# A two-layer relational graph network: memsets of 200 and 100 floats behind the gathers, one tile of 64 fetched row by row from SyncE, and another order of layer 1's last steps

## The chip, the cores and the metric

The kernel runs on one core of one Trainium2 chip. The metric is the device time of one execution, in microseconds (us), as the median over several runs. The engines of the core are PE (TensorE, matrix products), ACT (ScalarE), DVE (VectorE), POOL (GpSimd) and SP (SyncE, which here only issues DMAs). Each engine takes its instructions in program order and waits on semaphores for the others.

## What is computed

There are 12500 nodes with 128 features each and 200000 edges, sorted by destination; each edge has a source, a destination and one of 8 relation types. Two layers of a relational graph convolution are followed by a residual addition and a layer norm:

```python
def _rgcn_conv(x, src, dst, et, basis, comp, root, bias):
    W = jnp.einsum('rb,bio->rio', comp, basis)
    xw = jnp.einsum('ni,rio->nro', x, W)
    msgs = xw[src, et]
    seg = dst * N_REL + et
    summed = jax.ops.segment_sum(msgs, seg, num_segments=N_NODES * N_REL)
    cnt = jax.ops.segment_sum(jnp.ones((msgs.shape[0],), x.dtype), seg, num_segments=N_NODES * N_REL)
    mean = summed / jnp.maximum(cnt, 1.0)[:, None]
    agg = mean.reshape(N_NODES, N_REL, HIDDEN).sum(axis=1)
    return agg + x @ root + bias
...
h = x
for l in range(N_LAYERS):
    h = jax.nn.relu(_rgcn_conv(h, src, dst, et, basis[l], comp[l], root[l], bias[l])) + h
return _layernorm(x + h, axis=-1)
```

## The kernel before

The edges are cut into T = 1563 tiles of 128 edges, the tiles into NQ = 391 quads of four, and two quads make a group of eight tiles (NG = 196 groups). The 98 blocks of 128 nodes are the other measure of progress: about four quads feed one block.

**Layer 1** gathers, for each edge, its source's row of x (512 bytes). One indirect DMA on POOL brings the 128 rows of a tile (L583 in the function `gather`). PE multiplies each gathered tile with a one-hot matrix that DVE has written (`onehot`, L873; it holds the edges' weights too), which gives per-destination means transposed (`means`, L914); ACT copies them out. Per group PE applies the eight relation weights (`product`, L938) and places the result at its nodes (`place`, L961). When a block has all its edges, `close_block` adds the bias, takes the relu and the residual (L974 and after) and puts three steps on the list `todo`: a transposition, stored as hT_d, and two `half` steps that multiply the block with four of layer 2's relation weights each (L986). The products are stored as y_d, one row for each node and relation; both halves of a block are stored in one DMA. All these stores and loads are issued by SP (L565).

**Layer 2** gathers, for each edge, one row of y_d, by the index idy = source * 8 + type. PE multiplies the gathered tile with a one-hot matrix of 256 columns and accumulates straight into the block's sum (`add_rows`, L1028), to which it adds the root term. `finish` takes bias, relu and residual, `norm` transposes the block back and normalises it (L1062 to L1069), and SP stores the output. The gathers of layer 2 wait for all stores of y_d (L595).

**The memset.** Behind each gather POOL clears a part of a scratch tile `pace` (L589): 256 floats for each partition in layer 1, 200 in layer 2. Nothing reads it. Before that it waits for its own memset of eight gathers earlier.

**Order of the work.** The program is a list that is written out by hand: `Plan.add` takes each operation with the cells that it reads and writes, and derives the semaphore waits. Each engine executes its share of the list in that order, so an instruction that waits holds up everything behind it on its engine. The order comes from the loops over q at L1117 (layer 1) and L1166 (layer 2): in step q the gather of quad q + 12 is put on the list first (AHEAD = 12), into a ring of 14 quads, then DVE's one-hot of quad q + 2, then PE's work for quad q. The gathers use three lanes of semaphores in turn, the DMAs of SP eight. In the first part of layer 1 there is other work beside: DVE counts the edges per destination and type (`counts`, in pieces spread over the first steps) and computes the weights of layer 2.

After the loop of layer 1 stand its last steps (L1148 to L1158): place and close the last group but one, the product of the last group, the remaining `todo`, place and close the last block, its `todo`. The PSUM bank `pt` serves the transpositions and both halves of all blocks.

At the end SP waits for all DMAs, the engines meet (L1185, with a drain of each engine), each loads a flag `bad` (L1212), and a branch leads to another path for other inputs (L1213), which isn't taken here.

Of the kernel before, what the change touches and what calls it, by code (L numbers as in the profile page):

```python
# [8 lines left out]
F32 = mybir.dt.float32  # L9
# [3 lines left out]
ALU = mybir.AluOpType  # L13
# [402 lines left out]
def ordered_path(  # L416
# [21 lines left out]

    nc = tc.nc
    P = 128
    N, D = x.shape
# [16 lines left out]
    C = P + 2 * HALO  # L460
    S4 = 4
    AHEAD = 12
    H = R // 2
    assert D == P and R * K == P and B == BF + 1 and 1 < TL and LAST < P and BF % 4 == 0
    main = slice(HALO, HALO + P)

    const = ctx.enter_context(tc.tile_pool(name="const", bufs=1))
# [3 lines left out]
    def keep(shape, dtype, name):  # L471
        return const.tile(shape, dtype, name=name)
# [31 lines left out]
    sel = keep([P, G, K], F32, "sel")  # L504
    spread = keep([P, B, GB], F32, "spread")

    PACE, PACED = 8, (2 * P, 200)
    pace = keep([P, PACE, 2 * P], F32, "pace")
    paced = tc.alloc_semaphore("s_paced")
    key = keep([P, 4, C], F16, "key")  # L510
    low = keep([P, 4, C], I32, "low")
    eqs = Ring(const, 2, [P, S4, 4, C], F16, "eq")
    turns = Ring(const, 3, [P, 4, P], F32, "tu")
    rows_r = Ring(const, AHEAD + 2, [P, Q, D], F32, "rows")
    dm_r = Ring(const, 4, [P, Q, 2 * P], F32, "dm")
    sT_r = Ring(const, 3, [P, R, G, K], F32, "sT")
    pl_r = Ring(const, 3, [P, 2 * P], F32, "pl")
# [27 lines left out]
    o2 = keep([P, B], F32, "o2")  # L545
    nb_f = keep([1, 1], F32, "nb_f")

    plan = Plan(tc, {"hw": 8, "aq": 4, "gq": 3})
    plan.seen, plan.last = {}, {}

    def vec(emit, reads=(), writes=()):
# [5 lines left out]
    def pe(emit, reads=(), writes=()):  # L557
        plan.add("PE", emit, reads, writes)
# [8 lines left out]
    def copy(out_t, in_t, reads, writes):  # L567
        act(lambda: nc.scalar.activation(out_t, in_t, AF.Copy), reads, writes)  # L568

    rows_g = {}  # L570

    def gather(l, q):
        if q >= NQ:
            return
        t, cell = rows_r.take()
        rows_g[l, q] = (t, cell)
        ids = idx if l == 0 else idy

        def emit():
            ins = []  # L580
            for i in range(q * Q, min((q + 1) * Q, T)):
                m = LAST if i == T - 1 else P
                ins.append(nc.gpsimd.indirect_dma_start(  # L583
                    out=t[:m, i - q * Q, :], out_offset=None, in_=x if l == 0 else y_d,
                    in_offset=bass.IndirectOffsetOnAxis(ap=ids[:m, i:i + 1], axis=0)))
                k = l * T + i
                if k >= PACE:
                    nc.gpsimd.wait_ge(paced, k - PACE + 1)
                nc.gpsimd.memset(pace[:, k % PACE, :PACED[l]], 0).then_inc(paced, 1)  # L589
            return ins  # L590

        b = q * Q // P
        reads = ["idx0" if l == 0 and q == 0 else ("idx", b)] if l == 0 else [("idy", b)]
        if l == 1 and q == 0:
            reads += [("y_d", j) for j in range(NT)]  # L595
        plan.add("POOL", emit, reads, [cell], lane="gq", n=min(Q, T - q * Q))

    def weight(l, r):
        c0 = (l * R + r) * NB
# [280 lines left out]
    def load_block(j):  # L880
        if j >= NT:
            return
        n = rows_of(j)
        t, c = h_in[j] = hin_r.take()
        load(t[:n], x[j * P:j * P + n, :], [], [c])
# [20 lines left out]
    def means(q):  # L906
        t, c = rows_g.pop((0, q))
        d, dc = dms.pop((0, q))
        s, sc = s_b[q % 2]

        def emit():
            for i in range(in_quad(q)):
                m = LAST if q * Q + i == T - 1 else P
                last = nc.tensor.matmul(s[:, i, :], t[:m, i, :], d[:m, i, :P], start=True, stop=True)  # L914
            return last

        pe(emit, [c, dc], [sc])
        g = q * Q // G
        if g not in sT:
            sT[g] = sT_r.take()  # L920
        o, oc = sT[g]
        k0 = q * Q - g * G
        n = in_quad(q)
        copy(o[:, :, k0:k0 + n, :].rearrange("p r t k -> p t r k"),
             s[:, :n, :].rearrange("p t (r k) -> p t r k", k=K), [sc], [oc + (q % 2,)])
# [43 lines left out]
    def close_block(j):  # L969
        n = rows_of(j)  # L970
        p, pc = po[j]
        t, c = h_in.pop(j)
        h, hc = h_r.take()
        vec(lambda: nc.vector.tensor_add(h[:n], p[:n], bias_sb[:n]), [pc, "bias"], [hc])  # L974
        vec(lambda: nc.vector.scalar_tensor_tensor(h[:n], h[:n], 0.0, t[:n], op0=ALU.max, op1=ALU.add), [c], [hc])
        pt, pc2 = pt_b
        yc, ycc = yc_r.take()
        yr, yrc = yr_r.take()

        def turn():  # L980
            pe(lambda: nc.tensor.transpose(pt[:, 0, :n], h[:n, :], ident[:n, :n]), [hc, "ident"], [pc2])
            copy(yc[:, :n], pt[:, 0, :n], [pc2], [ycc])
            load(hT_d[j * P:(j + 1) * P, :n], yc[:, :n], [ycc], [("hT_d", j)])

        def half(k):
            pe(lambda: nc.tensor.matmul(pt[:n].rearrange("p r d -> p (r d)"), yc[:, :n],  # L986
                                        w_sb[:, 1, k * H:(k + 1) * H, :].rearrange("p r d -> p (r d)"),
                                        start=True, stop=True),
               [ycc] + [("w", 1, r) for r in range(k * H, (k + 1) * H)], [pc2])
            copy(yr[:n, k * H:(k + 1) * H, :], pt[:n], [pc2], [yrc + (k,)])  # L990
            if k == 1:
                load(y_d[j * P * R:(j * P + n) * R, :].rearrange("(p r) d -> p (r d)", r=R),
                     yr[:n].rearrange("p r d -> p (r d)"), [yrc + (0,), yrc + (1,)], [("y_d", j)])

        todo.extend([turn, lambda: half(0), lambda: half(1)])
# [7 lines left out]
             (ct_b[0].rearrange("p t d -> p (t d)")[:, :2 * P], ct_b[1])]  # L1003

    def load2(k):
        if not 0 <= k < NT:
            return
        n = rows_of(k)
        t, c = hTs[k] = hin_r.take()
        load(t[:, :n], hT_d[k * P:(k + 1) * P, :n], [("hT_d", k)], [c])  # L1010
        t, c = xs[k] = xs_r.take()
        load(t[:n], x[k * P:k * P + n, :], [], [c])

    def add_rows(q, k, opens, last):
        t, c = rows_g.pop((1, q))
        d, dc = dms.pop((1, q))
        a, ac = acc[k]
        n = in_quad(q)
        root_in = opens and k >= 0
        reads = [c, dc]  # L1020
        if root_in:
            ht, hc = hTs[k]
            reads += [hc, ("w", 1, R)]

        def emit():
            for i in range(n):
                m = LAST if q * Q + i == T - 1 else P
                ins = nc.tensor.matmul(a, t[:m, i, :], d[:m, i, :], start=(opens and i == 0),  # L1028
                                       stop=(last and i == n - 1))
                if i == 0 and root_in:  # L1030
                    nc.tensor.matmul(a[:, :rows_of(k)], w_sb[:, 1, R, :], ht[:, :rows_of(k)], start=False, stop=False)
            return ins

        pe(emit, reads, [ac])
# [60 lines left out]
        gather(0, q)  # L1095
    load_block(0)
    load_block(1)
    run(counts(0), 99)
    sources(*groups[1])
    turn_block(0)  # L1100
# [13 lines left out]
    later = [lambda b=b: check_edges(b) for b in range(B)]  # L1114
    later += [check_span, check_place, check_all]
    later.reverse()
    for q in range(NQ):  # L1117
        g = q * Q // G
        gather(0, q + AHEAD)
        onehot(0, q + 2)  # L1120
        if q == 1:
            where()
        if q % 2 == 0 and g > 0:
            place_in(g - 1)
        means(q)
        if q % 2 == 0:
            if g > 0:
                for j in fresh(g - 1):
                    open_block(j)
                product(g - 1)  # L1130
        else:
            if g > 0:
                for j in place(g - 1):
                    close_block(j)
            for j in fresh(g):
                if j not in hT:
                    turn_block(j)
                load_block(j + 1)
        if q % 4 != 3 and todo:
            todo.pop(0)()  # L1140
        if q < R:
            weight(1, q)
        if parts is not None:
            if run(parts, 2):
                parts = None
        elif later:
            later.pop()()
    g = NG - 1  # L1148
    for j in place(g - 1):
        close_block(j)  # L1150
    product(g)
    place_in(g)
    while todo:
        todo.pop(0)()
    for j in place(g):
        close_block(j)
    while todo:
# [2 lines left out]
    for q in range(AHEAD):  # L1160
        gather(1, q)
    load2(0)
    for q in range(2):
        onehot(1, q)
    due = []
    for q in range(NQ):  # L1166
        k = sup(q)
        gather(1, q + AHEAD)
        onehot(1, q + 2)
        opens = q == 0 or sup(q - 1) != k  # L1170
        last = q == NQ - 1 or sup(q + 1) != k
        if opens:
            acc[k] = acc_b[k % 3]
            load2(k + 1)
        add_rows(q, k, opens, last)
        for d in due:
            norm(d)
        due = []
        if last:
            finish(k)  # L1180
            due.append(k)
# [60 lines left out]
```

## Time and profile before

| | |
|---|---|
| median of 10 runs | 4499.05 us (4497.73 to 4502.11) |
| profiled execution | 4500.36 us; span of its instructions 4498.5 us |
| busy: POOL | 3929.1 us (87%) |
| busy: PE, its weight loads | 2758.6 us (61%), 2135.6 us (47%) |
| busy: DVE, ACT | 1711.0 us (38%), 518.7 us (12%) |
| DMA traffic | 295.88 MB, 66 GB/s |
| layer 1's gathers | first issued at 3.6 us, last at 2265.9 us |
| layer 2's gathers | first issued at 2289.8 us, last at 4470.2 us |

The profile is of one execution. In a group of instructions a row gives line, engine, operation, tiles written and read, shape, the count, then the busy time, the mean duration in ns, and the idle time of the engine just before them with what ended it ("issue" means that the engine waited for nothing that the profile shows). In order of time a row gives the start in us, the duration, the engine and, in brackets, the idle time ahead. "SPq" is SP's issuing of a DMA, not the transfer. In the list of waits the numbers are total us, times, and the longest. A row of one line's instructions gives shortest, median and longest duration in ns.

### The profile page before, as it was taken

What the parts mean: (1) busy time and instruction counts of PE and PEld (TensorE: products, weight loads), DVE (VectorE), ACT (ScalarE), POOL (GpSimd) and SP (SyncE); (2) the same over time, 40 slices, a digit from 0 to 9 for tenths busy, and PEclk for the clock granted to TensorE, in tenths of its full rate; (3) what the DMA queues carried; (4) which work ended last, traced back from release to release, by engine and by line L of the source; (5) the groups of instructions that cost most, each with busy time, mean ns of one, the idle gap of its engine ahead of it and who ended that gap; (6) DMA issues with size and microseconds to landing.
All of it is one profiled execution on the core that took longest, in us unless ns stands there. A gap on an engine that the chain in (4) does not pass through costs nothing.

```text
span 4498.5 us, 38109 instructions
## 1 busy us (share of the span) xinstructions
PE 2758.6 (61%) x11691; PEld 2135.6 (47%) x11691; DVE 1711.0 (38%) x4724; ACT 518.7 (12%) x1190; POOL 3929.1 (87%) x6260
## 2 busy tenths in 40 slices
PE   4786666666666666666665565565655556555554
PEld 3565555555555555555544344444444444444443
DVE  8772222222222222222234444444444444444343
ACT  0231211122111111121110000000000000000000
POOL 8888888888888888888878888888888888888886
PEclk7998888878888878888867766666667666666676
DMA  3222222222222222222222222222222222222221
GB/s 90 68 87 75 76 75 75 75 75 74 71 75 75 75 75 75 75 74 72 75 64 56 56 56 56 56 56 56 56 56 56 56 56 56 56 56 56 56 57 43
DMA packets 193416, 295.88 MB, mean 66 GB/s; under 512 B 60725, under 2 KB 130687, under 8 KB 193203
## 3 DMA queue, kind: packets, MB, share of 16 engines
q0 software_dynamic: 100032, 205.00, 17.5%
q1 hardware_dynamic: 90650, 86.62, 5.9%
q8 instruction: 96, 1.57, 0.2%
q10 hardware_dynamic: 2521, 1.73, 0.1%
q14 instruction: 117, 0.96, 0.1%
HBM read 229.11 MB, written 64.00 MB: 65 GB/s over the span
## 4 chain that ended last, share of the span: by engine, by line
POOL 72%; issue 10%; PE 9%; DVE 4%; DMA 4%; ACT 0%; POOLq 0%; ACTq 0%; DVEq 0%; SPq 0%
POOL rows L583 55%; POOL pace L589 17%; PE y L938 3%; DMA rows<-in_x_dram,idx 2%; PE s L914 2%; PE s L1028 2%; DMA rows<-y_d,idy 1%; DVE w_sb L607 1%; DVE dm L873 1%; PE ct L1028 1%; DVE eq L709 1%; PE ct L715 1%; PE ct L716 1%; PE pt L986 0%; DVE tu L732 0%
## 5 line engine op out<-in xcount | busy, mean ns | idle before, releaser
L583 POOL DMA_INDIRECT rows<-y_d,idy x1563 | 1486.9, 951 | 280.5 <-issue 254.8
L583 POOL DMA_INDIRECT rows<-in_x_dram,idx x1563 | 1495.4, 957 | 259.0 <-issue 250.3
L1028 PE MATMUL s<-dm,rows 128*128 128x256 f32 x2086 | 838.2, 565 | 595.7 <-DMA rows<-y_d,idy 444.7
L914 PE MATMUL s<-dm,rows 128*128 128x128 f32 x3126 | 539.5, 326 | 712.6 <-DMA rows<-in_x_dram,idx 712.1
L1028 PEld LDWEIGHTS s<-dm,rows 128*128 128x128 f32 x2086 | 558.3, 284 | 840.5 <-issue 459.5
L589 POOL MEMSET pace<- 128x256 f32 (+1 forms) x3126 | 953.0, 305 | 2.0
L914 PEld LDWEIGHTS s<-dm,rows 128*128 128x128 f32 x3126 | 466.9, 227 | 893.7 <-DMA rows<-in_x_dram,idx 760.9
L873 DVE TENSOR_SCALAR dm<-cols,near,w 128x256 f32<-128x256 f32 x1563 | 725.8, 533 | 56.7 <-PE ct L1028 28.8
L873 DVE TENSOR_SCALAR dm<-cols,kr,w 128x128 f32<-128x128 f32 x1563 | 531.3, 401 | 467.4 <-PE s L914 467.4
L1028 PE MATMUL ct<-dm,rows 128*128 128x256 f32 x1040 | 417.9, 565 | 307.5 <-DMA rows<-y_d,idy 231.5
L938 PE MATMUL y<-w_sb,sT 128*128 128x128 f32 x3136 | 566.6, 358 | 0.0
L938 PEld LDWEIGHTS y<-w_sb,sT 128*128 128x128 f32 x3136 | 557.8, 275 | 0.3 <-issue 0.2
L1028 PEld LDWEIGHTS ct<-dm,rows 128*128 128x128 f32 x1040 | 279.3, 285 | 429.9 <-issue 223.2
L974 DVE TENSOR_TENSOR h<-po,bias_sb 128x128 f32<-128x128 f32 x98 | 28.5, 290 | 947.3 <-PE po L961 947.3
L568 ACT ACTIVATE sT<-s 128x512 f32<-128x512 f32 x391 | 233.3, 597 | 1187.8 <-PE s L914 1187.8
L1047 DVE TENSOR_TENSOR y_col<-s,hT 128x128 f32<-128x128 f32 x66 | 19.2, 290 | 601.8 <-ACT hT L1040 601.8
L986 PE MATMUL pt<-w_sb,y_col 128*128 128x512 f32 x392 | 210.7, 620 | 2.1 <-ACT y_row L568 1.4
L1063 DVE TENSOR_TENSOR h<-po,xs 128x128 f32<-128x128 f32 x98 | 28.5, 291 | 308.3 <-PE po L1062 308.3
L1040 ACT ACTIVATE hT<-s,bias_t 128x128 f32<-128x128 f32 x65 | 23.9, 367 | 994.4 <-PE s L1028 994.4
L568 ACT ACTIVATE y_row<-pt 128x512 f32<-128x512 f32 x196 | 117.0, 597 | 140.9 <-PE pt L986 140.9
L961 PE MATMUL po<-ys,pl 128*128 128x128 f32 x780 | 119.7, 276 | 5.0 <-DVE pl L949 2.9
L1047 DVE TENSOR_TENSOR y_col<-ct,hT 128x128 f32<-128x128 f32 x32 | 9.3, 291 | 291.9 <-ACT hT L1040 291.9
(121 smaller groups left out, 1300.0 us busy)
## 6 DMA issues: line engine op xcount, KB each, us to landing
y_d<-y_row SPq DMA_DIRECT2D x97, 512.0 KB
rows<-in_x_dram,idx POOLq DMA_INDIRECT x1563
rows<-y_d,idy POOLq DMA_INDIRECT x1563
h_in<-in_x_dram SPq DMA_DIRECT2D x98, 64.0 KB
h_in<-hT_d SPq DMA_DIRECT2D x98, 64.0 KB
xs<-in_x_dram SPq DMA_DIRECT2D x98, 64.0 KB
hT_d<-y_col SPq DMA_DIRECT2D x97, 64.0 KB
out_dram<-ys SPq DMA_DIRECT2D x97, 64.0 KB
```

The source lines that it names most:

```text
L568: act(lambda: nc.scalar.activation(out_t, in_t, AF.Copy), reads, writes)
L583: ins.append(nc.gpsimd.indirect_dma_start(out=t[:m, i - q * Q, :], out_offset=None, in_=x if l == 0 else y_d, in_offset=bass.IndirectOffse ...
L589: nc.gpsimd.memset(pace[:, k % PACE, :PACED[l]], 0).then_inc(paced, 1)
L607: vec(lambda b=b: nc.vector.scalar_tensor_tensor(w_sb[:, l, r, :], b_sb[:, l, b, :], comp_sb[:, c0 + b:c0 + b + 1], w_sb[:, l, r, :], op0= ...
L709: vec(lambda s=s, eq=eq, s0=s0: nc.vector.tensor_tensor(eq[:, s - s0, :nb, HALO - s:HALO + P], key[:, :nb, HALO - s:HALO + P], key[:, :nb, ...
L715: nc.tensor.matmul(ct[:, :nb, :], id_h, eq[:, s - s0, :nb, main], start=(s == 1), stop=False)
L873: last = nc.vector.tensor_scalar(t[:, i - q * Q, :wide], cols[:, :wide], ids[:, i:i + 1], w[:, i:i + 1], op0=ALU.is_equal, op1=ALU.mult)
L914: last = nc.tensor.matmul(s[:, i, :], t[:m, i, :], d[:m, i, :P], start=True, stop=True)
L938: last = nc.tensor.matmul(y[:m], t[:, r, :nt, :].rearrange("p t k -> p (t k)"), w_sb[:, 0, r, :], start=(r == 0), stop=(r == R - 1))
L961: last = nc.tensor.matmul(po[j][0][:n], t[:m, k * P:k * P + n], o[:m], start=False, stop=(j in closed))
L986: pe(lambda: nc.tensor.matmul(pt[:n].rearrange("p r d -> p (r d)"), yc[:, :n], w_sb[:, 1, k * H:(k + 1) * H, :].rearrange("p r d -> p (r d)"),
L1028: ins = nc.tensor.matmul(a, t[:m, i, :], d[:m, i, :], start=(opens and i == 0), stop=(last and i == n - 1))
```

## The change

The memsets shrink from 256 to 200 floats in layer 1 and from 200 to 100 in layer 2.

One tile in 64 (tiles 63, 127, ..., 1535; 24 a layer) is no longer gathered by POOL. SP fetches its 128 rows, one DMA for each row: in each step q, `fetch` loads eight source numbers from `src_i` into eight registers of SP and issues eight DMAs of one row each ("a bite"); sixteen bites make a tile. The bite of step q belongs to the quad eight steps later (LEAD), the first eight bites of each layer stand ahead of its loop, and each waits for the bite four before it on its lane. The tile lies in a ring of two. PE's matmul of that tile reads this ring instead of `rows`. After the loop of layer 1 one DVE operation turns `src_i` into source * 8 + type for 1536 tiles; layer 2's bites load these numbers.

In the last steps of layer 1, the product, placing and closing of the last group but one, and the `todo` steps except one, now come before the means of the last quad (which the loop leaves out). For the last block only, the second half is multiplied into the bank `ct` instead of `pt` and copied by DVE instead of ACT, and each half is stored by its own DMA.

In layer 2 the loads of block 1 are put ahead of the loop, a drain of POOL is put behind the last gather, and in the last step the normalisation of the last block but one comes before the last quad's matmuls.

```diff
     AHEAD = 12
+    FAR, LEAD = 16, 8
+    BITE = P // FAR
     H = R // 2
-    assert D == P and R * K == P and B == BF + 1 and 1 < TL and LAST < P and BF % 4 == 0
+    assert D == P and R * K == P and B == BF + 1 and 1 < TL and LAST < P and BF % 4 == 0 and NQ % 2 == 1
     main = slice(HALO, HALO + P)
...
-    PACE, PACED = 8, (2 * P, 200)
+    PACE, PACED = 8, (200, 100)
     pace = keep([P, PACE, 2 * P], F32, "pace")
     paced = tc.alloc_semaphore("s_paced")
+    n_paced = [0]
     key = keep([P, 4, C], F16, "key")
...
     rows_r = Ring(const, AHEAD + 2, [P, Q, D], F32, "rows")
+    far_r = {e: Ring(const, 2, [P, D], F32, f"far{e}") for e in ("SP", "ACT")}
     dm_r = Ring(const, 4, [P, Q, 2 * P], F32, "dm")
...
-    plan = Plan(tc, {"hw": 8, "aq": 4, "gq": 3})
+    plan = Plan(tc, {"hw": 8, "aq": 4, "gq": 3, "rSP": 4, "rACT": 4})
+    far_at = {"SP": FAR - 1}
+    row_regs = {e: [plan.engines[e].alloc_register(f"row{k}") for k in range(BITE)] for e in far_at}
     plan.seen, plan.last = {}, {}
...
-    rows_g = {}
+    rows_g, far_g = {}, {}
+
+    def far(i):
+        for e, at in far_at.items():
+            if i % (FAR * Q) == at * Q + Q - 1 and i < BF * P and (at == FAR - 1 or i >= FAR * Q):
+                return e
+        return None
+
+    def fetch(e, l, q, part=0, parts=1):
+
+
+        s = q + LEAD + FAR - 1 - far_at[e]
+        i, c = (s // FAR * FAR + far_at[e]) * Q + Q - 1, s % FAR
+        if far(i) != e:
+            return
+        if c == 0 and part == 0:
+            far_g[l, i] = far_r[e].take()
+        t, cell = far_g[l, i]
+        n = BITE // parts
+        eng = plan.engines[e]
+        regs = row_regs[e]
+
+        def emit():
+            if part == 0:
+                eng.load(regs, src_i[i % P:i % P + 1, i // P, c * BITE:(c + 1) * BITE])
+            ins = []
+            for k in range(part * n, part * n + n):
+                at = eng.snap(regs[k], min_val=0, max_val=(N if l == 0 else N * R) - 1)
+                p = c * BITE + k
+                ins.append(eng.dma_start(t[p:p + 1, :], (x if l == 0 else y_d)[bass.ds(at, 1), :]))
+            return ins
+
+        reads = [("src", i // P)]
+        if l == 1 and i < 2 * FAR * Q:
+            reads += [("y_d", j) for j in range(NT)] + [("y_d", NT - 1, 1)]
+        plan.add(e, emit, reads, [cell + (c, part)], lane="r" + e, n=n)
+
+    def bits(l, i):
+        return [far_g[l, i][1] + (c, part) for c in range(FAR) for part in range(2)] if far(i) else []
...
+        tiles = [i for i in range(q * Q, min((q + 1) * Q, T)) if not far(i)]
+
...
             ins = []
-            for i in range(q * Q, min((q + 1) * Q, T)):
+            for i in tiles:
                 m = LAST if i == T - 1 else P
...
                     in_offset=bass.IndirectOffsetOnAxis(ap=ids[:m, i:i + 1], axis=0)))
-                k = l * T + i
+                k = n_paced[0]
+                n_paced[0] += 1
                 if k >= PACE:
...
         if l == 1 and q == 0:
-            reads += [("y_d", j) for j in range(NT)]
-        plan.add("POOL", emit, reads, [cell], lane="gq", n=min(Q, T - q * Q))
+            reads += [("y_d", j) for j in range(NT)] + [("y_d", NT - 1, 1)]
+        plan.add("POOL", emit, reads, [cell], lane="gq", n=len(tiles))
...
                 m = LAST if q * Q + i == T - 1 else P
-                last = nc.tensor.matmul(s[:, i, :], t[:m, i, :], d[:m, i, :P], start=True, stop=True)
+                rows = far_g[0, q * Q + i][0] if far(q * Q + i) else t[:, i, :]
+                last = nc.tensor.matmul(s[:, i, :], rows[:m], d[:m, i, :P], start=True, stop=True)
             return last
-        pe(emit, [c, dc], [sc])
+        pe(emit, [c, dc] + bits(0, q * Q + Q - 1), [sc])
         g = q * Q // G
...
         def half(k):
-            pe(lambda: nc.tensor.matmul(pt[:n].rearrange("p r d -> p (r d)"), yc[:, :n],
+            hb, hc2 = ct_b if j == NT - 1 and k == 1 else pt_b
+            pe(lambda: nc.tensor.matmul(hb[:n].rearrange("p r d -> p (r d)"), yc[:, :n],
                                         w_sb[:, 1, k * H:(k + 1) * H, :].rearrange("p r d -> p (r d)"),
                                         start=True, stop=True),
-               [ycc] + [("w", 1, r) for r in range(k * H, (k + 1) * H)], [pc2])
-            copy(yr[:n, k * H:(k + 1) * H, :], pt[:n], [pc2], [yrc + (k,)])
+               [ycc] + [("w", 1, r) for r in range(k * H, (k + 1) * H)], [hc2])
+            if j == NT - 1:
+                if k == 0:
+                    copy(yr[:n, :H, :], hb[:n], [hc2], [yrc + (k,)])
+                else:
+                    vec(lambda: nc.vector.tensor_copy(yr[:n, H:, :], hb[:n]), [hc2], [yrc + (k,)])
+                load(y_d[j * P * R:(j * P + n) * R, :].rearrange("(p r) d -> p r d", r=R)[:, k * H:(k + 1) * H, :],
+                     yr[:n, k * H:(k + 1) * H, :], [yrc + (k,)], [("y_d", j) if k == 0 else ("y_d", j, 1)])
+                return
+            copy(yr[:n, k * H:(k + 1) * H, :], hb[:n], [hc2], [yrc + (k,)])
             if k == 1:
...
     def load2(k):
-        if not 0 <= k < NT:
+        if not 0 <= k < NT or k in hTs:
             return
...
         root_in = opens and k >= 0
-        reads = [c, dc]
+        reads = [c, dc] + bits(1, q * Q + Q - 1)
         if root_in:
...
                 m = LAST if q * Q + i == T - 1 else P
-                ins = nc.tensor.matmul(a, t[:m, i, :], d[:m, i, :], start=(opens and i == 0),
+                rows = far_g[1, q * Q + i][0] if far(q * Q + i) else t[:, i, :]
+                ins = nc.tensor.matmul(a, rows[:m], d[:m, i, :], start=(opens and i == 0),
                                        stop=(last and i == n - 1))
...
     load_block(1)
+    for s in range(LEAD):
+        fetch("SP", 0, s - LEAD)
     run(counts(0), 99)
...
     later.reverse()
-    for q in range(NQ):
+    for q in range(NQ - 1):
         g = q * Q // G
         gather(0, q + AHEAD)
+        fetch("SP", 0, q)
         onehot(0, q + 2)
...
             later.pop()()
+    srcs = [("src", b) for b in range(BF)]
+    vec(lambda: nc.vector.scalar_tensor_tensor(src_i[:, :BF], src_i[:, :BF], float(R), ex[:, :BF, main], op0=ALU.mult,
+                                               op1=ALU.add),
+        ends("ex", 0, BF) + [("ex", 0, n) for n in (1, 2, 3)] + srcs, srcs)
     g = NG - 1
+    while todo:
+        todo.pop(0)()
+    place_in(g - 1)
+    for j in fresh(g - 1):
+        open_block(j)
+    product(g - 1)
     for j in place(g - 1):
         close_block(j)
+    place_in(g)
+    while len(todo) > 1:
+        todo.pop(0)()
+    means(NQ - 1)
+    todo.pop(0)()
     product(g)
-    place_in(g)
-    while todo:
-        todo.pop(0)()
     for j in place(g):
...
     load2(0)
+    load2(1)
+    for s in range(LEAD):
+        fetch("SP", 1, s - LEAD)
     for q in range(2):
...
         gather(1, q + AHEAD)
+        if q + AHEAD == NQ - 1:
+            pool(lambda: nc.gpsimd.drain())
+        fetch("SP", 1, q)
         onehot(1, q + 2)
...
             load2(k + 1)
-        add_rows(q, k, opens, last)
+        if q < NQ - 1:
+            add_rows(q, k, opens, last)
         for d in due:
...
         due = []
+        if q == NQ - 1:
+            add_rows(q, k, opens, last)
         if last:
...
             due.append(k)
```

## The prediction

> **What bounds the kernel now.** I read the page first (busy time, then the chain that ended last), then the groups of instructions with their shapes kept apart, then POOL in order of time.
>
> ```profile
> span 4498.5 us, 38109 instructions
> POOL 72%; issue 10%; PE 9%; DVE 4%; DMA 4%; ACT 0%; POOLq 0%; ACTq 0%; DVEq 0%; SPq 0%
> L583 POOL DMA_INDIRECT rows<-in_x_dram,idx x1563 | 1495.4, 957 | 259.0 <-issue 250.3 <-PE y L938 6.1 <-DMA idx<-in_src_dram 1.6
> L583 POOL DMA_INDIRECT rows<-y_d,idy x1563 | 1486.9, 951 | 280.5 <-issue 254.8 <-DMA y_d<-y_row 22.6 <-PE po L1062 3.1
> L589 POOL MEMSET pace<- 128x256 f32 x1563 | 513.5, 329 | 1.0
> L589 POOL MEMSET pace<- 128x200 f32 x1563 | 439.5, 281 | 1.0
> PE s L914 <- DMA rows<-in_x_dram,idx: 712.1, 290, 4.4
> PE s L1028 <- DMA rows<-y_d,idy: 444.7, 194, 3.8
> ```
>
> The chain is POOL for 72%, with most of the 10% "issue" between POOL's instructions. PE waits for gathered rows in both layers (712 and 445 us), so it follows the gathers. POOL's work is one strict alternation; in order of time, a piece of layer 1 and a piece of layer 2:
>
> ```profile
> 1000.18 0.95 POOL L583 DMA_INDIRECT rows<-in_x_dram,idx  x1 [0.17 <-issue]
> 1001.13 0.33 POOL L589 MEMSET pace<- 128x256 f32 x1
> ...
> 3000.19 0.95 POOL L583 DMA_INDIRECT rows<-y_d,idy  x1 [0.17 <-issue]
> 3001.14 0.28 POOL L589 MEMSET pace<- 128x200 f32 x1
> 3001.59 0.95 POOL L583 DMA_INDIRECT rows<-y_d,idy  x1 [0.17 <-issue]
> ```
>
> The gather takes 0.95 us and the idle time ahead of it 0.17 us, whether 256 or 200 floats are cleared between. The memset is therefore paid in full: a tile costs 957 + 329 + 166 (259.0 / 1563) = 1452 ns in layer 1, and 951 + 281 + 165 ((280.5 - 22.6) / 1563) = 1397 ns in layer 2.
>
> **The change, part by part.** All sums are against the profiled execution (4500.36 us; its span is 4498.5); the median of the ten runs, 4499.05, lies 1.3 us lower, which is taken off at the end. A difference of 0.2% (9 us) is about the least that a measurement of this kernel tells from none.
>
> *Memsets.* From 256 to 200 floats the duration falls by 48 ns; from the rows' busy times, (513.5 - 439.5) / 1563 = 47.3 ns for 56 floats, 0.845 ns a float. At 200 in layer 1 the row is there: 281 ns. At 100 no row exists; the nearest below is a memset of one float:
>
> ```profile
> 0.24 0.10 POOL L1228 MEMSET const-float32-0.0<- 128x1 f32 x1 [0.24 <-issue]
> ```
>
> So the bounds are 100 and 281 ns; the line through 256 and 200 gives 281 - 84.5 = 197 ns, and ends at 113 ns for one float, near the 100 measured, so I take 197. Layer 1 saves 1539 x 47.3 ns = 73 us, layer 2 1539 x 84.5 ns = 130 us (1539 gathers a layer remain). If nothing is given back elsewhere these lie on the chain.
>
> *One tile of 64 off POOL.* Tiles 63, 127, ..., 1535 are 24 in each layer. POOL loses 24 x 1.452 = 35 us and 24 x 1.397 = 34 us. SP gains, for each quad of tiles, one register load and eight DMAs of one row. The rows of SP that come nearest:
>
> ```profile
> 0.96 0.45 SPq L565 DMA_DIRECT2D idx<-in_src_dram  x1
> 1.46 0.40 SPq L565 DMA_DIRECT2D ex<-in_edge_type_dram  x1
> 4.27 0.26 SPq L565 DMA_DIRECT2D src_i<-in_src_dram  x1
> L1212 SPq TENSOR_LOAD <-bad x1: 462/462/462, 4491.7 to 4491.7; - x1
> L1212 SPq FUSED_REGOPS  x1: 191/191/191, 4496.3 to 4496.3; - x1
> L1212 SPq SEQ_ASSERT  x1: 32/32/32, 4496.5 to 4496.5; - x1
> ```
>
> The second and third are DMAs of one row each (704 and 256 bytes): 0.26 to 0.40 us, with about 0.05 us to the next (0.96 + 0.45 to 1.46). No row shows a DMA whose address sits in a register. From below its addition is nothing, from above a register operation and an assertion each time, 0.22 us. The load of eight registers lies between one load of one register, 0.46 us, and eight of them, 3.7 us. A "bite" of eight rows thus costs between 8 x 0.31 + 0.46 = 2.9 us and 8 x (0.45 + 0.05 + 0.22) + 3.7 = 9.5 us. I take 4.2: eight times (0.33 + 0.05 + 0.05) plus 0.8, because the row's offset is one scaling of a register and the eight numbers lie side by side. What else SP does for a block of 128 nodes:
>
> ```profile
> 1008.36 0.32 SPq L565 DMA_DIRECT2D y_d<-y_row  x1
> 1008.73 0.43 SPq L565 DMA_DIRECT2D h_in<-in_x_dram  x1
> ...
> 2335.13 0.34 SPq L565 DMA_DIRECT2D out_dram<-ys  x1
> 2335.51 0.43 SPq L565 DMA_DIRECT2D h_in<-hT_d  x1
> 2335.99 0.43 SPq L565 DMA_DIRECT2D xs<-in_x_dram  x1
> ```
>
> About 1.3 us a block, 130 us a layer. With 384 bites of 4.2 us a layer is 1613 + 130 = 1743 us of SP, against some 2020 us of gathers in the new layer 2 (1539 x 1.313). SP is then 86% full, and a bite is issued eight quads (over 40 us) ahead of its use, so it stays hidden. Queued behind a bite on SP are the stores of y_d, hT_d and the outputs and the loads of h_in and xs; each comes up to 4 us later. At the start of layer 2 eight bites stand together (34 us): loads for the third block come late there and PE may fall behind by some 10 to 20 us, but POOL fills its ring of 14 quads meanwhile (72 us of gathers), and PE's waits leave room to catch up. PE's extra wait for the bites comes once in 16 quads. Cover gone, this is the first rival.
>
> *The start of layer 1.* There POOL is not alone on the path. The windows of the gathered rows' tile, first 240 us:
>
> ```profile
> core 0: us, PE busy (x) PEld busy (x) POOL busy (x), PEclk, DMA share, GB/s
> 0.00:240.00 240.00, 30.14 (x208) 29.29 (x208) 158.07 (x159) 0.86 0.28 77
> ```
>
> 159 gathers are out and PE has used 104 tiles (two matmuls each): a lead of 55 in a ring that holds 56. A faster POOL meets the end of the ring, and what it gained by then, 159 x 47 ns + 2 tiles x 1.45 us = 10 us, is lost. I charge 10 us.
>
> *Layer 1's last steps.* POOL in order of time, and pieces of the chain of waits between:
>
> ```profile
> 2266.84 0.33 POOL L589 MEMSET pace<- 128x256 f32 x1
> 2289.77 0.96 POOL L583 DMA_INDIRECT rows<-y_d,idy  x1 [22.60 <-DMA y_d<-y_row]
> ...
> 2265.92 2.39 DMA rows<-in_x_dram,idx
> 2269.48 3.42 PE y L938 x16
> 2283.38 2.02 PE pt L986 x2
> 2286.04 2.98 DMA y_d<-y_row
> ```
>
> POOL idles 22.6 us. The product of 3.4 us, with the placing and closing behind it, waits behind the last quad's matmuls on PE; after the change it goes ahead of them, into time in which PE waited for the rows. The very last block's second half goes to another PSUM bank and to DVE, so one ACT copy (0.6 us) leaves the chain. PE's work stays and is now the chain, so I take 3.3 us, between 0 and 6. New there is one DVE operation on 1536 columns:
>
> ```profile
> L736 DVE SCALAR_TENSOR_TENSOR tu<-src_i,ex 128x512 f32<-128x512 int32 x3 | 2.0, 662 | 0.0
> ```
>
> Three times 0.66 us is 2 us, while DVE waits for PE; it costs nothing unless a last gather is held up for as long.
>
> *The end.* The drain of POOL, and who waits for it:
>
> ```profile
> 4471.15 0.28 POOL L589 MEMSET pace<- 128x200 f32 x1
> L1185 POOLq DRAIN  x1: 8477/8477/8477, 4483.1 to 4483.1; - x1
> SPq L1185 <- POOLq L1185: 8.3, 1, 8.3
> ```
>
> POOL is idle from 4471.4 to 4483.1 and then drains for 8.5 us with everything waiting. The change drains behind the last gather; 4471.4 + 8.5 = 4479.9 is before 4483.1, so 8.3 us go, if the second drain finds nothing left (0 to 8.3). Moving the last block but one's normalisation ahead of the last matmuls is worth 1 us at most; I take 1.
>
> **Sum.** Layer 1: 73 + 35 - 10 = 98. Between layers 3. Layer 2: 130 + 34 = 164. End 9. Together 274 us: 4500.4 - 274 = 4226, less 1.3 for the median: 4225 us.
>
> **Rivals.**
>
> *SP becomes the bound (slower).* In-order SP sets the pace once 384 bites and 130 us exceed layer 2's 2020 us: from 4.9 us a bite. At 5.0 the layer takes 2050 us, the kernel some 4255. At 6.0 both layers take 384 x 6.0 + 130 = 2434 us, with 40 us of ends 4910 us. It equals the kernel before at about 5.5. For it: the bounds (2.9 to 9.5) straddle the point, and nothing shows the register-addressed form. Against: the short one-row DMAs, and that most of a bite is plain issue. A little over the line (4.9 to 5.4 us): 0.06; beyond: 0.11. [...] No run here shows a load of several registers.
>
> *The memset hides work of POOL.* If something behind the gather takes as long as the 446 ns (281 + 165) that now follow it in layer 2, a shorter memset only lengthens the idle time or the gather. Then layer 2 gives back 130 us (4355 us), and if the same holds at 256, layer 1 too (4428 us). For it: gaps under 446 ns appear nowhere. Against: from 495 to 446 ns neither row moved. 0.13. [...]
>
> *The change does nothing:* SP's late rows cost what POOL gains, within 9 us of 4499; it needs the first rival at just that price. 0.02.
>
> **How the numbers follow.** The forecast has 0.68; its own range is 4200 to 4260 (the 100-float memset 20 ns either way is 31 us; ends and ring 10). To hold 8 in 10 the range reaches up to 4365, which takes in SP a little over its line and the lost memset of layer 2. Faster: 0.68 + 0.13 + 0.06 = 0.87; the same 0.02; slower 0.11.
>
> **What would show it.** Right: memset rows of about 281 and 197 ns, gathers still at 951 with 0.17 us idle, x1539 each; PE still waiting for gathered rows; SP's bites under 4.9 us from start to start of work; a short last drain; a gap between layers of about 20 us. Wrong: PE waiting for the row-wise tile and SP never idle (first rival); a longer gather or idle time ahead of it (second); a POOL that waits for PE long past 300 us.

## The result and the profile after

The changed kernel takes 4227.72 us, median of 8 runs (4226.29 to 4229.42); the kernel before takes 4500.07 us beside it. The ratio is 0.9395, 95% interval 0.9387 to 0.9403. The profiled execution took 4225.47 us, with a span of 4223.7.

One thing has to be said before the experiments: they did not all run on a chip like that of this result. There, and in one experiment, the kernel before takes 4499 to 4500 us; I call that A. In the other eleven experiments it takes 4583 to 4584 us; I call that B. B was met on the chips numbered 2 and 0, the experiment on A ran on number 7, and the number of the result's chip is not known; "chip" stands below for a chip with all that belongs to it. Comparisons are within one of the two, unless both are named.

First the page and the groups of instructions of the changed kernel on A (line, engine, operation, count, busy time, mean ns, idle time ahead), then three rows of its list of PE's waits (total us, times, longest):

```profile
span 4223.7 us, 57294 instructions
POOL 69%; issue 12%; PE 6%; DMA 4%; DVE 4%; SPq 4%; ACT 0%; POOLq 0%; ACTq 0%; DVEq 0%
L630 POOL DMA_INDIRECT rows<-in_x_dram,idx x1539 | 1474.8, 958 | 263.7 <-issue 247.4 <-PE s L963 10.9 <-PE y L987 1.8
L630 POOL DMA_INDIRECT rows<-y_d,idy x1539 | 1463.4, 951 | 272.0 <-issue 242.9 <-DMA y_d<-y_row 18.5 <-DMA rows<-y_d,idy 6.3
L637 POOL MEMSET pace<- 128x200 f32 x1539 | 432.8, 281 | 0.9
L637 POOL MEMSET pace<- 128x100 f32 x1539 | 304.5, 198 | 0.9
PE s L963 <- DMA rows<-in_x_dram,idx: 578.7, 247, 4.5
PE s L1087 <- DMA rows<-y_d,idy: 415.7, 186, 3.6
PE pt L940 <- DMA h_in<-in_x_dram: 81.4, 15, 7.3
```

POOL still sets the end, the gathers are as long as before, only the memsets have shrunk, and PE still waits for gathered rows. The last row is new: in the kernel before PE waited 1.1 us for these loads of SP, and the chain held SP for 0% instead of 4%. What SP now does, by line (shortest, median, longest ns; first and last start):

```profile
L601 SPq TENSOR_LOAD <-src_i x768: 708/796/1628, 18.2 to 4134.5; - x192
L604 SPq FUSED_REGOPS  x6144: 44/44/60, 18.9 to 4138.8; - x199
L606 SPq DMA_DIRECT2D farSP<-y_d x3072: 224/228/298, 2189.2 to 4138.9; - x192
```

And the rows that bound the stretches, in order of time, with the two drains of POOL:

```profile
2170.26 0.28 POOL L637 MEMSET pace<- 128x200 f32 x1
2189.05 0.96 POOL L630 DMA_INDIRECT rows<-y_d,idy  x1 [18.51 <-DMA y_d<-y_row]
...
4207.43 0.20 POOL L637 MEMSET pace<- 128x100 f32 x1
L1247 POOLq DRAIN  x1: 15808/15808/15808, 4199.8 to 4199.8; - x1
L1268 POOLq DRAIN  x1: 41/41/41, 4216.1 to 4216.1; - x1
```

Cut at the same places as the rows of before (end of layer 1's last memset, first gather of layer 2, end of its last memset, end of the span), the 274.8 us come from here:

| stretch | before | after | gain | predicted |
|---|---|---|---|---|
| layer 1 | 2267.17 | 2170.54 | 96.6 | 98 |
| between the layers | 22.60 | 18.51 | 4.1 | 3.3 |
| layer 2 | 2181.66 | 2018.58 | 163.1 | 164 |
| after the last memset | 27.07 | 16.07 | 11.0 | 9 |

### The profile page after: what moved, and what is told of

It is laid out like the page before. It is cut to its first block, busy times and chain, and to the rows that moved or that the text cites. A ratio compares the mean times of both kernels' runs of the same rounds, so it can differ in the third digit from the quotient of the medians.

```text
span 4223.7 us, 57294 instructions
## 1 busy us (share of the span) xinstructions
PE 2586.5 (61%) x11691; PEld 2027.1 (48%) x11691; DVE 1714.5 (41%) x4726; ACT 518.8 (12%) x1189; POOL 3669.2 (87%) x6164
## 4 chain that ended last, share of the span: by engine, by line
POOL 69%; issue 12%; PE 6%; DMA 4%; DVE 4%; SPq 4%; ACT 0%; POOLq 0%; ACTq 0%; DVEq 0%
POOL rows L630 56%; POOL pace L637 14%; DMA rows<-y_d,idy 3%; SPq L606 2%; PE s L1087 1%; PE y L987 1%; DVE dm L921 1%; PE s L963 1%; SPq L601 1%; DMA rows<-in_x_dram,idx 1%; DVE w_sb L655 1%; DVE eq L757 1%; PE ct L1087 1%; PE ct L763 1%; PE ct L764 1%
## 5 line engine op out<-in xcount | busy, mean ns | idle before, releaser
L630 POOL DMA_INDIRECT rows<-in_x_dram,idx x1539 | 1474.8, 958 | 263.7 <-issue 247.4
L630 POOL DMA_INDIRECT rows<-y_d,idy x1539 | 1463.4, 951 | 272.0 <-issue 242.9
L1087 PE MATMUL s<-dm,rows 128*128 128x256 f32 x2054 | 751.1, 522 | 575.3 <-DMA rows<-y_d,idy 415.7
L1087 PEld LDWEIGHTS s<-dm,rows 128*128 128x128 f32 x2054 | 506.2, 262 | 785.3 <-issue 366.9
L963 PE MATMUL s<-dm,rows 128*128 128x128 f32 x3078 | 520.9, 322 | 582.0 <-DMA rows<-in_x_dram,idx 578.7
L963 PEld LDWEIGHTS s<-dm,rows 128*128 128x128 f32 x3078 | 458.0, 225 | 749.8 <-DMA rows<-in_x_dram,idx 636.0
L637 POOL MEMSET pace<- 128x200 f32 (+1 forms) x3078 | 737.2, 240 | 1.8
L1087 PE MATMUL ct<-dm,rows 128*128 128x256 f32 x1024 | 372.9, 521 | 289.7 <-DMA rows<-y_d,idy 208.4
L987 PE MATMUL y<-w_sb,sT 128*128 128x128 f32 x3136 | 538.3, 345 | 0.0
L987 PEld LDWEIGHTS y<-w_sb,sT 128*128 128x128 f32 x3136 | 529.2, 262 | 1.2 <-ACT sT L575 0.8
L1087 PEld LDWEIGHTS ct<-dm,rows 128*128 128x128 f32 x1024 | 252.1, 261 | 395.4 <-issue 195.1
```

Source lines behind the costliest of these rows:

```text
L630: ins.append(nc.gpsimd.indirect_dma_start(out=t[:m, i - q * Q, :], out_offset=None, in_=x if l == 0 else y_d, in_offset=bass.IndirectOffse ...
L963: last = nc.tensor.matmul(s[:, i, :], rows[:m], d[:m, i, :P], start=True, stop=True)
L987: last = nc.tensor.matmul(y[:m], t[:, r, :nt, :].rearrange("p t k -> p (t k)"), w_sb[:, 0, r, :], start=(r == 0), stop=(r == R - 1))
L1087: ins = nc.tensor.matmul(a, rows[:m], d[:m, i, :], start=(opens and i == 0), stop=(last and i == n - 1))
```

## The experiments

The theory was the prediction's sum: POOL paces both layers, and each nanosecond taken off its alternation counts. Its rivals were the prediction's own, and later that the chip decides.

**The memsets alone, and the rest without them.** Two kernels take the change apart (before with the new sizes; after with the old), two push the memset further.

```diff
e1_memsets, in the kernel before
-    PACE, PACED = 8, (2 * P, 200)
+    PACE, PACED = 8, (200, 100)
e2_old_memsets, in the changed kernel
-    PACE, PACED = 8, (200, 100)
+    PACE, PACED = 8, (2 * P, 200)
e3_one_float, in the kernel before
-    PACE, PACED = 8, (2 * P, 200)
+    PACE, PACED = 8, (1, 1)
e4_no_memset, in the kernel before
-                if k >= PACE:
-                    nc.gpsimd.wait_ge(paced, k - PACE + 1)
-                nc.gpsimd.memset(pace[:, k % PACE, :PACED[l]], 0).then_inc(paced, 1)
```

> The kernel before with the memsets of 200 and 100 floats as its only edit. Theory (the memset is paid in full, nothing gives it back): 73 + 130 = 203 us less, of which some 8 us are lost to the full ring at the start of layer 1, so about 4305 us; gather rows stay at 951 ns with 0.17 us of idle time ahead. Rival (the memset covers work of POOL that has to be done anyway): the idle time or the gather grows by what the memset loses, 4370 to 4500 us.

> The changed kernel with the memsets of before (256 and 200 floats), all its other edits kept. Theory: the row-wise tiles, the last steps and the drain alone are worth 35 + 34 + 3 + 9 = 81 us less a little for the ring, so about 4422 us, and the memsets' 203 us of the result are missing. Rival (SP's bites cost what they save): 4480 us or more.

> The kernel before with memsets of one float in both layers. Theory (memset paid in full down to its shortest, about 113 ns): 1563 x 216 ns + 1563 x 168 ns = 600 us less, some 15 to 30 us of it lost to the ring and to PE in layer 1: 3915 to 3930 us; gathers at 951 ns. Rival (there is hidden work behind the gather that is longer than the shortest memset): gather or idle time grows, the sum of gather, memset and idle time stays over 1.23 us, and the time lies between 3950 and 4300 us.

> The kernel before without memset and without its wait: gather follows gather. Theory (memset is pure cost): a tile takes 951 ns plus at most 0.17 us, so 3126 x 1.12 us + 60 us = 3560 us, or what PE then sets, 3600 to 3800 us. Rival (the memset keeps something slow from happening between two gathers): the gathers' own row is longer than 951 ns or idle time grows, and the time comes out above that of one float, 3950 us or more.

Measured, on B (before 4582.88 us): 4601.25 us (ratio 1.0047, 1.003 to 1.0064), 4864.63 (1.062, 1.0580 to 1.0659), 4651.08 (1.0155, 1.0136 to 1.0174) and 4643.86 (1.0136, 1.0115 to 1.0157). All four miss the sum, by 296 us and more. The groups of the one-float kernel and two rows of POOL's order of time in the kernel without memsets say where the sum does hold:

```profile
L583 POOL DMA_INDIRECT rows<-in_x_dram,idx x1563 | 1487.4, 952 | 664.5 <-issue 275.6 <-PE s L914 156.6 <-remote 153.9
L583 POOL DMA_INDIRECT rows<-y_d,idy x1563 | 1474.7, 944 | 615.7 <-issue 295.5 <-remote 250.3 <-DMA y_d<-y_row 53.8
L589 POOL MEMSET pace<- 128x1 f32 x3126 | 363.6, 116 | 5.4 <-issue 3.0 <-remote 0.5 <-POOL pace L589 0.2
```

```profile
3003.67 0.94 POOL L583 DMA_INDIRECT rows<-y_d,idy  x1 [0.30 <-issue]
3004.92 0.94 POOL L583 DMA_INDIRECT rows<-y_d,idy  x1 [0.30 <-issue]
```

Behind a memset of 116 ns, and behind none at all, a gather is not longer than before: 944 to 952 ns. From one to the next it is 1.25 us either way (with no memset the idle time is 0.30 us, so a memset of one float is free). The rival that the memset hides POOL's work is out, down to a period of 1.25 us. But POOL loses what it gains: the first group holds 157 us of waits for PE (6.1 in the kernel before on A), and both hold waits for releasers that the profile doesn't know ("remote").

**Chip or edit?** The two kernels of the case as they are, the memsets again, and the memsets with a slow beginning.

```diff
c4_slow_start, in e1_memsets
-                nc.gpsimd.memset(pace[:, k % PACE, :PACED[l]], 0).then_inc(paced, 1)
+                nc.gpsimd.memset(pace[:, k % PACE, :2 * P if k < 640 else PACED[l]], 0).then_inc(paced, 1)
```

> The changed kernel as it is, beside the four edits of the first call, whose kernel before took 4583 us and not 4500. If the chip decides (theory: TensorE, at the clock that this chip grants, can't take a tile in less than 1.42 us, and POOL runs into its full ring): PE a ring behind POOL as in the edits, TensorE gaps of about 21 us every two blocks, about 4400 to 4600 us. If the edit decides (rival: the whole change keeps TensorE close behind POOL where a half of it doesn't): 4228 us, PE 2 to 5 tiles behind, no gaps over 8 us.

> The kernel before as it is, for its profile on this chip. If the chip decides: where it takes 4583 us, PE a ring behind POOL in part of the span, gaps in TensorE, POOL periods over 1441 and 1395 ns in the mean; where it takes 4500 us, none of this. If the edit decides: the same profile as before on any chip.

> The memsets of 200 and 100 floats alone, once more. If the chip decides: 4305 us where the kernel before takes 4500 us, 4600 us where it takes 4583 us. If the edit decides: 4600 us on any chip.

> The memsets of 200 and 100 floats alone, but the first 640 gathers of layer 1 keep 256 floats, so that TensorE catches up with POOL at the old pace before the new one begins. If falling behind at the start is what keeps TensorE a ring behind (rival): about 4335 us (4305 + 640 x 0.047), lag 2 to 5 tiles from 450 us on. If TensorE's clock sets the floor of 1.42 us a tile: within 0.5% of the memsets alone.

Measured, all on B (before 4584.22 us): the changed kernel 5320.16 us (1.1602, 1.1575 to 1.1628), the kernel before 4580.94 (0.9993, 0.998 to 1.0006), the memsets 4600.61 (1.0041, 1.0027 to 1.0055), the slow start 4588.04 (1.0011, 1.0001 to 1.0021). So the chip decides, and by more than I had allowed: the same change that takes 6% off on A adds 16% on B, outside both numbers that I had given for the changed kernel. The slow start gains 13 us. It doesn't do what it was meant to: under its long memsets PE is still 25 to 41 tiles behind (300 to 930 us), and 42 to 53 after them. That the start isn't the reason is seen in the kernel before on B: after the pause between the layers PE is level with POOL (2300 us), and 35 tiles behind 200 us later, at the old pace.

The expectations gave TensorE's clock as the reason for a floor of 1.42 us a tile. The floor is there: without row tiles, layer 2's gathers on B come every 1.42 us in the mean with memsets of 200, 100 and 1 floats and with none. The clock is not the reason: between 2500 and 4000 us it is 0.73 in the kernel before on B and 0.68 on A, and a matmul of 256 columns takes 475 ns on B (into `s`) against 565 on A.

The changed kernel on B: the chain, SP's rows as above, and PE's waits.

```profile
SPq 55%; issue 34%; PE 6%; DVE 3%; another core or an unknown queue 1%; ACT 0%; DMA 0%; ACTq 0%; DVEq 0%
L601 SPq TENSOR_LOAD <-src_i x768: 2/763/1621, 18.2 to 5280.7; - x192
L604 SPq FUSED_REGOPS  x6144: 1/44/1393, 19.0 to 5284.9; - x199
L606 SPq DMA_DIRECT2D farSP<-in_x_dram x3072: 1/227/775, 19.5 to 2369.9; - x192
L606 SPq DMA_DIRECT2D farSP<-y_d x3072: 1/228/1395, 2420.1 to 5285.1; - x192
PE s L1087 <- DMA h_in<-hT_d: 1159.0, 60, 21.3
PE ct L1087 <- DMA h_in<-hT_d: 636.0, 30, 68.5
```

The chain is SP in place of POOL, and PE waits 1795 us for loads of h_in, which stand behind the bites in SP's queue. From one bite to the next it is (2369.9 - 19.5) / 384 = 6.1 us in layer 1 and (5285.1 - 2420.1) / 384 = 7.5 us in layer 2. Most of that is the bite itself: from the start of its load to the end of its last row's issue it takes 5.7 and 7.1 us in the mean (on A 4.3 in both), and SP waits for other engines for only some 120 us in all. That is the prediction's first rival, past its 4.9 us. The medians of the single instructions are near those of A. What differs is that some are held: a register operation of 44 ns takes up to 1393 ns (on A up to 60). Others are recorded with 1 ns, so a single duration on B is not to be relied on. In order of time, SP's row DMAs in the changed kernel on A, then SP and POOL of the same kernel on B:

```profile
2999.84 15.29 SPq L606 DMA_DIRECT2D farSP<-y_d  x30
```

```profile
3000.20 15.82 SPq L606 DMA_DIRECT2D farSP<-y_d  x14
3018.41 5.67 SPq L606 DMA_DIRECT2D farSP<-y_d  x11
...
3012.72 0.95 POOL L630 DMA_INDIRECT rows<-y_d,idy  x1 [0.17 <-issue]
3013.67 0.20 POOL L637 MEMSET pace<- 128x100 f32 x1
3022.67 0.95 POOL L630 DMA_INDIRECT rows<-y_d,idy  x1 [8.81 <-PE po L1121]
```

SP issues 14 rows in 15.8 us, of which POOL gathers 13.7 without a stop; then, for the most part while POOL waits (3013.9 to 3022.7), 11 in 5.7 us, about A's pace. Over all of layer 2, from one row DMA to the next the median is 0.93 us where gathers started within 1.5 us on both sides (0.75 inside a bite) and 0.42 us elsewhere; on A it is 0.42 us with gathers running.

The kernel with the memsets alone has no bites, and there it is PE that stops. PE, ACT and POOL in order of time, on B:

```profile
3007.70 1.50 PE L1028 MATMUL s<-dm,rows 128*128 128x256 f32 x6
3028.80 0.37 ACT L1040 ACTIVATE hT<-ct,bias_t 128x128 f32<-128x128 f32 x1 [28.39 <-remote]
3029.87 0.47 PE L1062 MATMUL po<-ident,y_col 128*128 128x128 f32 x1 [20.66 <-DVE y_col L1048]
...
3024.22 0.95 POOL L583 DMA_INDIRECT rows<-y_d,idy  x1 [0.17 <-issue]
3029.03 0.95 POOL L583 DMA_INDIRECT rows<-y_d,idy  x1 [3.67 <-remote]
```

The block's matmuls are recorded as issued by 3009; ACT, which needs their sum, starts at 3028.8, after POOL, at the end of its ring, had ceased at 3025.4; then PE, ACT and POOL all go on. After the first 100 us, more than 8 us pass from one matmul's start to the next 73 times (1245 us in all); in the kernel before on B 61 times (880 us), on A once, between the layers. So PE stays 41 to 53 tiles behind POOL (gathers ended less tiles used) from 600 us to the end of layer 1 and 28 to 46 in layer 2 from 2500 us on; on A it is mostly 1 to 5 behind from 600 us on, in the kernel before and in the changed one. On B a faster POOL fills the ring and waits: for PE's first matmuls of a quad in layer 1 (L914) it waited 2.1 us in the kernel before, 36.8 with memsets of 200 and 100 floats and 156.6 with one float.

**The row tiles taken out, on A.**

```diff
g1_no_rows, in the changed kernel
-    far_at = {"SP": FAR - 1}
+    far_at = {}
...
+        if e not in far_at:
+            return
         s = q + LEAD + FAR - 1 - far_at[e]
```

> The changed kernel with its row-by-row tiles given back to the gathers (3,126 gathers again, nothing on SyncE but its loads and stores); the memsets of 200 and 100 floats, the new order of layer 1's last steps and the early drain stay. Where the kernel before takes 4500 us: the terms of the sum add up (theory) to 4228 + 24 x 1.395 + 24 x 1.311 = 4293 us; below 4260 or above 4330 speaks for a tie between the parts (rival). Where the kernel before takes 4584 us and the changed kernel 5320 us: if it is SyncE's row instructions, held 0.7 us at a time, that set that time (theory), 4580 to 4610 us as for the memsets alone; if it is the new order, the earlier drain or the loads (rival), still above 5000 us.

Measured, on A (before 4499.19 us): 4289.27 us, ratio 0.9534 (0.9519 to 0.955), 4 us from the sum. Its rows at the same four places (its span is 4287.3 us):

```profile
2200.35 0.28 POOL L639 MEMSET pace<- 128x200 f32 x1
2220.70 0.96 POOL L632 DMA_INDIRECT rows<-y_d,idy  x1 [20.07 <-DMA y_d<-y_row]
...
4270.20 0.20 POOL L639 MEMSET pace<- 128x100 f32 x1
```

Layer 2 is 2049.7 us, 132.0 less than before, which is 1563 times 84.5 ns to the microsecond. Layer 1 is 66.5 us shorter, against 1563 x 47.3 ns = 74; the 7 us less I put down to the ring at the start, which no run separates. The row tiles bring the rest: 30.1 us in layer 1, 31.1 in layer 2, 2.4 at the ends. On A the parts add up; the memsets alone were never measured there, so no run excludes that they need the new order beside them.

**Once more the memsets, one float, and a dearer bite.**

```diff
h1_memsets, in the kernel before: as e1_memsets
h2_one_float, in the changed kernel
-    PACE, PACED = 8, (200, 100)
+    PACE, PACED = 8, (1, 1)
h3_twelve_rows, in the changed kernel
+    spare = keep([P, 4, D], F32, "spare")
...
                 ins.append(eng.dma_start(t[p:p + 1, :], (x if l == 0 else y_d)[bass.ds(at, 1), :]))
+                if k % 2:
+                    ins.append(eng.dma_start(spare[p:p + 1, k // 2, :], (x if l == 0 else y_d)[bass.ds(at, 1), :]))
...
-        plan.add(e, emit, reads, [cell + (c, part)], lane="r" + e, n=n)
+        plan.add(e, emit, reads, [cell + (c, part)], lane="r" + e, n=n + n // 2)
```

> The kernel before with memsets of 200 and 100 floats and nothing else, a third time. Where the kernel before takes 4500 us, the terms add up (theory): 4289 us (the kernel without the row tiles) plus the ends and the new order, some 12 to 16 us: 4301 to 4305. If the new order is what lets the shorter memsets act (rival): 4400 to 4600. Where the kernel before takes 4584 us: 4600 as twice before.

> The changed kernel with memsets of one float in both layers. If the memsets only space the gathers (theory), POOL's period falls to the 1.249 us of the one-float kernel before: 4228 - 1539 x (1.395 - 1.249) - 1539 x (1.311 - 1.249) = 3908 us, with SyncE then at 384 x 4.2 + 130 = 1743 us of 1922 a layer. If TensorE can't follow at that pace (rival): a lag of a whole ring, POOL waiting for TensorE, no gain below 4150. If the memsets hide POOL's own work (second rival of the prediction): gathers over 950 ns and above 4100.

> The changed kernel with every second row of a row-by-row tile fetched once more, into a spare tile: twelve row DMAs a bite in place of eight. A bite then takes about 4.2 + 4 x 0.28 = 5.3 us. If SyncE bounds the kernel from 4.9 us a bite (first rival of the prediction, theory for the 5320 us): 384 x 5.3 + 130 = 2165 us a layer, so layer 2 grows by 146 us and layer 1 by about nothing: about 4375 us, SyncE without waits in layer 2. If SyncE has more room than that (rival): 4228 us.

These again ran on B (before 4583.09 us): 4601.60 us (1.0042, 1.0029 to 1.0056), 5709.05 (1.2462, 1.2416 to 1.2508) and 6200.52 (1.354, 1.3507 to 1.3573). The chain of the twelve-row kernel and its largest wait of PE:

```profile
SPq 52%; issue 29%; PE 11%; another core or an unknown queue 5%; DMA 1%; DVE 1%; ACT 1%; POOL 1%; POOLq 0%; ACTq 0%
PE s L1090 <- DMA h_in<-hT_d: 1526.8, 62, 27.3
```

For A these two numbers say nothing, and the 3908 us for one float on A stays untried. For B they are one more test of SP as the bound: four more DMAs a bite cost 880 us over the changed kernel, 1.15 us a bite, which is 4 x 0.29 us, so each microsecond put on SP came out in the end (had SP had room, as in the sum that I made for A, layer 1 would have cost nothing). With one float POOL could gather faster; SP's rows are then 1.42 us apart while POOL gathers (1.20 inside a bite), 0.42 us otherwise, and the kernel is 389 us slower than the changed one. With the rows the time on B rises as the memset shrinks, 4865, 5320, 5709 us; without them it hardly moves, 4583, 4601, 4651. That the gathers hold the other engines up on B fits both series; no run held the gathers still while all else ran, so it is inferred from order and from these series, not shown by itself. For PE, the floor of 1.42 us a tile at any pace of POOL would fit as well a price that has nothing to do with the gathers.

## Why the prediction was right, and where it was not

On A the sum came out, and the total is 2.7 us off.

- Memsets: predicted 281 and 197 ns, measured 281 and 198; paid in full, as the run without row tiles shows for layer 2 alone.
- Row tiles: predicted 69 us off POOL, of the spans 63.6. I had priced the 24 tiles at the old periods (1.452 and 1.397 us) beside memsets already shrunk. At the new ones (1.395 and 1.311) it is 65. The rest is missing in layer 1, where POOL waits 10.9 us for PE's matmuls, nearly all in the first 240 us (4.9 without the row tiles).
- The bite: predicted 4.2 us with a load of 0.8. The load of eight registers is 796 ns, 100 ns a register, and 30 rows with their loads in 15.29 us make 4.1 us for eight.
- "It stays hidden": on A this holds for the time, not for all of the way. From 240 to 520 us PE waits 79.5 us for loads of h_in that stand behind bites in SP's queue, where in the kernel before it waited 72.9 us for gathered rows. At 400 us it is still 19 tiles behind POOL, against 4 in the kernel before and without the row tiles. So for a time SP, not POOL, set PE's pace. PE stayed inside the ring of 56 tiles, and after 240 us no wait of POOL for it was longer than 0.2 us, about its usual idle time; that is why the total doesn't show it.
- The ring at the start: 10 us charged; with it layer 1's gain came out 1.4 us under the sum.
- Between the layers: 3.3 predicted, 4.1 measured. The DVE operation that I called free takes 1.7 us. The one gather beside it took 1.83 us instead of 0.95 (1.65 in the run without row tiles); that costs 0.9 us, but in layer 1, not here:

```profile
L1211 DVE SCALAR_TENSOR_TENSOR src_i<-src_i,ex 128x1536 int32<-128x1536 int32 x1 | 1.7, 1745 | 0.0
2160.11 1.83 POOL L630 DMA_INDIRECT rows<-in_x_dram,idx  x1 [0.17 <-issue]
```

- The second rival: on A the gathers stay at 951 to 958 ns with 0.16 us of idle time ahead, and on B at 944 to 952 ns with one float or nothing cleared behind them, so the memset hid no work of POOL down to a period of 1.31 us on A and 1.25 on B. On A a gather's rows arrive after its record has ended: one that starts at 3087.57 us is recorded for 0.95 us, and the chain of waits gives 2.53 us to the end of its transfer. The next two start at 3088.88 and 3090.19 us with the same 0.17 us of idle time ahead, so neither was held by it.
- The end: 9 predicted, 11.0 measured. The drain ends at 4215.6, 0.5 us before the engines meet, and the second takes 41 ns, as assumed.
- The median: I took 1.3 us off because the profiled execution of before lay above its median; that of the changed kernel lies 2.3 us under its own.

On B the step that fails is the bite of 4.2 us, by which SP was "86% full" and stayed hidden. With the bites as measured from load to last row, the rival's formula gives 384 x (5.66 + 7.05) + 2 x 130 + 40 = 5181 us, 139 below the 5320 measured; SP's waits for other engines are 120 of these. (The spacing of 6.1 and 7.5 us contains those waits and would only give the span again.) The rival had the right place and the right point of decision; I had looked for it in the price of SP's instructions, and it lay in their being held. The trace of before on A, on which I argued, showed little of the kind: after the first 100 us 20 of SP's 586 DMAs took more than 460 ns to issue, the longest 1452, all of them loads. The second step that fails there is "paid in full": with PE a ring behind, time taken off POOL is waited away again.

The change brings 6% on a chip that behaves like A and costs 16% on one that behaves like B. On B shorter memsets alone did not pay: 4601 us with 200 and 100 floats, 4651 with one, 4644 with none, against 4583.

## What to carry to other kernels

Time taken off the engine that paced this kernel counted in full where those behind it followed (132.0 us of layer 2 on A, with PE mostly 1 to 5 tiles behind), and not where they didn't (18 us lost with the shorter memsets alone on B, with PE 28 to 53 tiles behind over most of both layers). Look at how far they lag (tiles gathered less tiles used): on B a full ring turned the whole saving into waiting. Work moved to an idle queue wants room there for more than its price on one trace (a bite of 4.3 us on A took 7.1 on B), so look first at the loads that already stand in that queue: in layer 1 PE waited 81.4 us for h_in on A, against 1.1 before, where the total didn't show it, and 404.6 us on B. One trace shows one chip: where a forecast leans on an in-order queue being 86% full, a second chip is worth more than a finer estimate.

## What the runs showed of the hardware

- On A a DMA of one row with its address in a register takes SP 228 ns to issue, 0.42 us from row to row with its register work, and eight registers are loaded in 0.80 us.
- POOL's drain ends 8.0 us after the last memset (4207.6 to 4215.6), and took 8.5 us in the kernel before, where POOL had been idle for 11.7 us ahead of it. So waiting before it did not shorten it; here an earlier place hid it.
- TensorE's granted clock rose in layer 2 with POOL's faster pace on A, from 0.68 (2500 to 4000 us, before) to 0.77, in the changed kernel and without the row tiles alike. No cause was looked for.
- What holds SP and PE on B is open. One trait of the traces stands beside it: for the kernel before they contain 67,312 semaphore updates on A and 20,656 on B, though the program is the same. No run here shows a link from missing records to holds.
